# Smaller pieces of tensor work between the attention steps, and small vector work gathered in every fourth step

## The chip, the core and the metric

The kernel runs on one core of one Trainium2 chip. The metric is the device time of one execution in microseconds (us), the median of several runs. The kernel before takes 1864.74 us (three runs, 1863.59 to 1865.54). One execution was profiled as well: it took 1867.24 us, and its recorded span is 1865.5 us.

A core has engines that each run their own instructions strictly in the order in which the program lists them, and that wait for one another only through semaphores: PE (TensorE, matrix products; PEld is its loading of weights), DVE (VectorE), ACT (ScalarE), POOL (GpSimd) and SP (SyncE, which here only issues DMA transfers). Matrix products land in PSUM, a small memory of eight banks.

## What is computed

The reference is a block of cross attention and a feed-forward part whose weights come from a table of 16 values. Cut to what matters:

```python
# x: (16, 256, 512), ctx: (16, 256, 512), mask: (16, 1, 512), float32
xn = layernorm(x)                                   # over the last axis
q = einsum('oc,bct->bot', Wq, xn) + bq              # 16 heads of 16 rows
k = einsum('oc,bcs->bos', Wk, ctx) + bk
v = einsum('oc,bcs->bos', Wv, ctx) + bv
dot = einsum('bhdt,bhds->bhts', q, k) / 4
m = mask[:, :, :, None] * mask[:, :, None, :]
a = softmax(m * dot - (1 - m) * 1e6, -1) * m
x = x + einsum('bhts,bhds->bhdt', a, v).reshape(16, 256, 512)
y = layernorm(x)
gate, up = y @ lut[gate_idx].T, y @ lut[up_idx].T   # 512 -> 1376
x = x + (silu(gate) * up) @ lut[down_idx].T         # 1376 -> 512
```

## The kernel before

The attention is cut into 64 units `u` of four heads each; two units make a group `k` (half of the 256 channels of one batch element `b`, so two groups make a batch element). A unit has eight steps, and the whole attention is one loop over steps `s`, from -46 to 513, with the order written out by hand. One step lists, in this order:

1. `scores_max(s + 16)`: two products `pa` of 512 columns for the unit that is two ahead, and one DVE reduction of their 1024 columns (L476), which gives the row maxima.
2. what the list `between[s]` holds, which `pe(...)` fills: work with matrix products in it.
3. `scores_exp(s)`: two products `pb` and one ACT exponential of 1024 columns (L493).
4. what the list `after[s]` holds, which `at(...)` fills: other work.
5. `looked.fill(...)`: some DVE instructions of the table look-up of the weights, counted in credits; a look-up instruction on 512 columns costs 0.15 + 512/1250 = 0.56 credits. The attention loop carries eight look-ups of 19 such instructions, which use up their credits near step 355.

Since an engine keeps the listed order, an instruction that waits holds back everything listed behind it on its engine. `pa` and `pb` share a pool of three PSUM tiles, taken in turn: `pb` of step n+1 takes the tile of `pa` of step n, so it waits for that reduction, and `pa` of step n+2 takes the tile of `pb` of step n, so it waits for that exponential. All other products of the attention use one bank, `ps_m`, and the output of a unit one more.

Work of a group `k`, with t = 16k, counted in steps: the products of q and k (`project`, two of 512 columns each), evicted by ACT, multiplied by the mask on POOL (L388), split into a high and a low part by ACT and POOL (`halve`, L394 and L396), written to memory by SP (`stage`) and fetched back in another layout into one of four QK tiles (`fetch_unit`); the products of v (`project_v`, four of 256 columns), evicted by ACT (L444), and then on POOL two additions of the bias (L447) and four products with the mask (L454). A unit's maxima are split on DVE (`halve_max`, L499 and L500), turned on PE (`turn_max`) and sent into the QK tile by POOL (`send_max`). The exponentials are multiplied with v by `apply_v`, in steps 8u+5 and 8u+9, so in every step with s % 4 == 1: these are the steps with products of v. After them come, per group, the sums and their inverse (`take_sums`, `load_sums`, `invert` on DVE, `send_sums`, `spread_sums`), the rows' end on POOL (`finish_rows`: L574 and L575), the statistics of the second layer norm on DVE (`stats2`: L92 and L93, then four small POOL instructions L97 to L100), the normalised rows on POOL (`norm2`, L593), their four transposes on PE (`turn_rows`, L600) and the stores. `stats1` and `norm1` do the first layer norm of a batch element, every second group.

Two steps are equal if they differ by 16, so the place of all this is best read as s mod 16. Before the change `finish_rows` stands in step 7, `stats2` in step 9, the last piece of `project_v` in step 12.

In the steps below 0 the first groups are prepared and the QK tiles filled; the feed-forward part follows the loop.

Of the kernel before, what the change touches and what calls it, by code (L numbers as in the profile page):

```python
# [9 lines left out]
F32 = mybir.dt.float32  # L10
# [10 lines left out]
def kernel(  # L21
# [17 lines left out]
    nc = tc.nc  # L39
    P = 128  # L40
    B, C, T = x.shape
# [7 lines left out]
    NCC = C // P  # L49
    NK = B * NCC  # L50
    NU = 2 * NK
    NH = T // P
    NO = (INTER + P - 1) // P
    NB = NK // 4
    AHEAD = 16
    NSTEP = 8 * NU
    PARTS = ((0, 4 * P), (4 * P, 8 * P), (8 * P, INTER))
    NP = NO // 2
    HALF = T // 2
# [7 lines left out]
    ps_m = ctx.enter_context(tc.tile_pool(name="ps_m", bufs=1, space=PSUM))  # L67
# [19 lines left out]
    def words(t):  # L87
        return t.bitcast(F32)
# [146 lines left out]
    with ExitStack() as att:  # L235
# [9 lines left out]
        wv = ac.tile([P, NCC, C], F32, tag="wv", name="wv")  # L245
# [5 lines left out]
        m_d = dpool.tile([B, 4, 2, T], F32, tag="m_d", name="m_d")  # L251
# [47 lines left out]
        m8 = early.tile([P, 4, 2, T], F32, tag="m8", name="m8")[:B]  # L299
# [37 lines left out]
        def send_mask():  # L337
            nc.vector.tensor_copy(m8[:, 2:4, 0, :], m8[:, 0:2, 0, :])
            nc.vector.tensor_copy(m8[:, 1:4:2, 1, :], m8[:, 0:4:2, 1, :])

        def fill_tiles():
            nc.sync.dma_start(m_d, m8)
            for t in vas:
                nc.vector.memset(t, 1.0)
            nc.vector.memset(words(Ks[1]), 1.0)
# [21 lines left out]

        nat, parts = {}, {}

        def project(k, which, o):  # L370
            b, oc = divmod(k, NCC)
            cx, xn, mb = inp[b][:3]
            w, src_t = (wk, cx) if which == "k" else (wq, xn)
            if o == 0:
                parts[which] = ps_m.tile([P, 512], F32, tag="m", name=f"p{which}_{k}")
            ps = parts[which]
            nc.tensor.matmul(  # L377
                ps, w[:, o, oc, :], src_t[:, o, :], start=(o == 0), stop=(o == NCC - 1)
            )
            if o < NCC - 1:  # L380
                return
            t = p1.tile([P, T], F32, tag=f"nat{which}", name=f"nat{which}_{k}")
            if which == "k":
                nc.scalar.activation(t, ps, AF.Identity, bias=bkc[:, oc : oc + 1])  # L384
            else:
                nc.scalar.activation(t, ps, AF.Identity, bias=bqc[:, oc : oc + 1], scale=QK)  # L386
            eng = nc.vector if k == 0 else nc.gpsimd
            eng.tensor_tensor(t, t, mb, ALU.mult)  # L388
            nat[which, k] = t
# [36 lines left out]
                nat.pop(("q", k))  # L426
                nat.pop(("k", k))

        def project_v(k, i):
            b, half = divmod(k, 2)  # L430
            cx = inp[b][0]
            if i == 0:
                parts["v"] = ps_m.tile([P, 512], F32, tag="m", name=f"pv_{b}_{half}")
            ps = parts["v"]
            c = 2 * half + i
            for o in range(NCC):
                nc.tensor.matmul(  # L437
                    ps[:, i * C : (i + 1) * C], cx[:, o, c * P : (c + 1) * P], wv[:, o, :],
                    start=(o == 0), stop=(o == NCC - 1),
                )  # L440
            if i == 0:
                return
            vt = p1.tile([P, 2, C], F32, tag="vt", name=f"vt_{b}_{half}")
            nc.scalar.copy(vt, ps.rearrange("p (c n) -> p c n", n=C))  # L444
            va = vas[b % 2]
            for cc in range(2):
                nc.gpsimd.tensor_tensor(vt[:, cc], vt[:, cc], bvb, ALU.add)  # L447
            for cc in range(2):
                c = 2 * half + cc
                m = mcol[:, b * NCH + c : b * NCH + c + 1]  # L450
                v4 = vt[:, cc].rearrange("p (h e d) -> p e h d", e=2, d=D)
                a4 = va[:, c].rearrange("p (h e) d -> p e h d", e=2)
                for e in range(2):
                    nc.gpsimd.tensor_scalar(  # L454
                        a4[:, e, :, 16 * e : 16 * e + 16], v4[:, e], m, None, ALU.mult
                    )
# [75 lines left out]
        dens, rbs, rows2 = {}, {}, {}  # L532
# [60 lines left out]
            nc.gpsimd.tensor_scalar(xn, u, rstd, nmr, ALU.mult, ALU.add)  # L593
            rows2[k] = xn

        def turn_rows(k):
            xn = rows2.pop(k)
            pt = ps_m.tile([P, 512], F32, tag="m", name=f"pt_{k}")
            for h in range(NH):
                nc.tensor.transpose(  # L600
                    pt[:, h * P : (h + 1) * P], xn[:, h * P : (h + 1) * P], ident
                )
            xt = rpool.tile([P, T], F32, tag="xt", name=f"xt_{k}")
            nc.scalar.copy(xt, pt)
            rows2[k] = xt
# [9 lines left out]
        def at(s, fn, *args):  # L615
            after[s].append(lambda: fn(*args))

        def pe(s, fn, *args):
            between[s].append(lambda: fn(*args))

        for u in range(NU):
            for c in range(NCH):
                pe(8 * u + 5 + 4 * (c // 2), apply_v, u, c)
        for k in range(NK):
            t = 16 * k
            for i in range(2):
                pe(t - 46 + 2 * i, project, k, "k", i)
                pe(t - 42 + 2 * i, project, k, "q", i)
                pe(t - 22 + 2 * i, project_v, k, i)
            at(t - 41, halve, k, "k")  # L630
            at(t - 37, halve, k, "q")
            at(t - 37, stage, k, "k")
            at(t - 33, stage, k, "q")
            for e in range(2):
                u = 2 * k + e
                at(8 * u - 23, fetch_unit, u)
                at(8 * u - 8, halve_max, u)
                pe(8 * u - 7, turn_max, u)
                at(8 * u - 6, send_max, u)
            at(t + 12, take_sums, k, 0)  # L640
            at(t + 20, take_sums, k, 1)
            at(t + 20, merge, k)
            at(t + 24, load_sums, k)
            at(t + 28, invert, k)
            at(t + 29, send_sums, k)
            at(t + 34, spread_sums, k)
            at(t + 39, finish_rows, k)
            at(t + 41, stats2, k)
            at(t + 42, send_rows, k)
            at(t + 42, norm2, k)  # L650
            pe(t + 47, turn_rows, k)
            at(t + 50, send_turned, k)
        for b in range(1, B):
            at(max(-22, 32 * b - 58), load_b, b)
            at(max(-14, 32 * b - 50), stats1, b)
            at(max(-13, 32 * b - 48), norm1, b, nc.gpsimd)
        for h in range(8):
            at(2 * h - 13, spread_mask, h)

        at(-43, halve_mask, 0)  # L660
        at(-41, halve_mask, 1)
        at(-39, send_mask)
        at(-32, fill_tiles)
        pe(-31, turn_mask)
        at(-29, rest_of_constants)

        right.close()
        lp = right.enter_context(tc.tile_pool(name="lookup", bufs=1, side="right"))
        looked = Lookups(lp, [weight_job(*w) for w in wpieces[:8]])
        xms, ws = [None] * NM, {}  # L670

        for s in range(min(between), NSTEP + 2):
            if 0 <= s + AHEAD < NSTEP:
                scores_max(s + AHEAD)
            for fn in between.pop(s, ()):
                fn()
            if 0 <= s < NSTEP:
                scores_exp(s)
            for fn in after.pop(s, ()):
                fn()  # L680
            if 0 <= s < NSTEP - AHEAD - 4:
                looked.fill(0.24)
            if s == NSTEP - AHEAD - 4:
                looked.rest()
                right.close()
                rx = ctx.enter_context(
                    tc.tile_pool(name="first", bufs=1, side="right", reuse_waits="tile")
                )
                xms[0] = rx.tile([P, 2, 4, NH, P], F32, tag="x0", name="x_0")
            if s in (NSTEP - 14, NSTEP - 13):  # L690
                k = s - NSTEP + 14
                nc.sync.dma_start(xms[0][:, k], xT_d[k])
            if s in (NSTEP - 11, NSTEP - 10):
                load_w(rx, s - NSTEP + 11)
# [5 lines left out]
    with ExitStack() as ffn:  # L700
        ps = ffn.enter_context(
            tc.tile_pool(name="ps_ff", bufs=7, space=PSUM, reuse_waits="tile")
        )
# [9 lines left out]
        def down_job(o):  # L713
# [16 lines left out]
        looked = Lookups(  # L730
            lp, [weight_job(*w) for w in wpieces[8:]] + [down_job(o) for o in range(NO)]
        )
# [209 lines left out]
        for n, (p, m) in enumerate(order):  # L942
# [36 lines left out]
            q = max(p, 1) + 1  # L979
# [142 lines left out]
```

## Time and profile before

| what | value |
|---|---|
| median of three runs | 1864.74 us |
| the profiled execution, its own time | 1867.24 us |
| its span | 1865.5 us |
| steps below 0 | up to about 57 us |
| attention steps | about 57 to 1057 us |
| feed-forward part | about 1057 to 1865 us |
| DVE reduction of `pa` (L476) | 512 times, mean 1219 ns |
| ACT exponential (L493) | 512 times, mean 1024 ns |
| granted TensorE clock, mean | 0.996 |

The view of windows gives, for a stretch of the span, how long each engine was busy and the granted TensorE clock (1.00 is full speed). The timeline lists instructions by start, with the idle time of their engine before them and what ended it in brackets; instructions that follow each other closely are merged into one row, and matrix products overlap, so distances are best taken from start to start. The view of waits sums the idle times by what ended them.

### The profile page before, as it was taken

What the parts mean: (1) busy time and instruction counts of PE and PEld (TensorE: products, weight loads), DVE (VectorE), ACT (ScalarE), POOL (GpSimd) and SP (SyncE); (2) the same over time, 40 slices, a digit from 0 to 9 for tenths busy, and PEclk for the clock granted to TensorE, in tenths of its full rate; (3) what the DMA queues carried; (4) which work ended last, traced back from release to release, by engine and by line L of the source; (5) the groups of instructions that cost most, each with busy time, mean ns of one, the idle gap of its engine ahead of it and who ended that gap; (6) DMA issues with size and microseconds to landing.
All of it is one profiled execution on the core that took longest, in us unless ns stands there. A gap on an engine that the chain in (4) does not pass through costs nothing.

```text
span 1865.5 us, 21778 instructions
## 1 busy us (share of the span) xinstructions
PE 1792.9 (96%) x7281; PEld 990.9 (53%) x7281; DVE 1354.4 (73%) x1882; ACT 807.7 (43%) x1103; POOL 672.5 (36%) x918
## 2 busy tenths in 40 slices
PE   5999999999999999999999999999999999999999
PEld 2455555545554555555554444444444443888888
DVE  7889888888888888877777588878888844323222
ACT  1566666666666666666666622222222222000000
POOL 5546565656665566656554220000000000111111
PEclk9999999999999999999999999999999999999999
DMA  7655667676667667665755633122222215543521
GB/s 195 163 141 154 169 184 165 168 182 170 160 171 184 168 150 172 183 168 146 171 147 117 234 124 107 66 93 77 92 74 85 75 60 200 190 156 116 189 69 45
DMA packets 117807, 264.88 MB, mean 142 GB/s; under 512 B 25920, under 2 KB 35072, under 8 KB 107312
## 3 DMA queue, kind: packets, MB, share of 16 engines
q1 hardware_dynamic: 103680, 249.04, 46.4%
q0 software_dynamic: 12672, 12.94, 3.8%
q10 hardware_dynamic: 1344, 1.52, 0.3%
q8 instruction: 58, 0.95, 0.2%
q14 instruction: 53, 0.43, 0.1%
HBM read 167.06 MB, written 91.03 MB: 138 GB/s over the span
## 4 chain that ended last, share of the span: by engine, by line
PE 76%; DVE 10%; ACT 6%; DMA 5%; issue 2%; SPq 0%; POOL 0%; ACTq 0%; DVEq 0%
PE pv L523 10%; PE pb L489 9%; PE pa L472 9%; PE pb_g L737 6%; PE pb L737 6%; ACT pt L493 6%; PE pb_u L737 5%; PE px L737 4%; DVE nm L476 4%; PE pe L737 4%; PE pa_g L737 4%; PE pe_g L737 4%; PE pe_u L737 4%; PE pa_u L737 3%; PE pk L377 3%; DMA QK<-dk 2%
## 5 line engine op out<-in xcount | busy, mean ns | idle before, releaser
L476 DVE TENSOR_REDUCE nm<-pa 128x2 f32<-128x1024 f32 x512 | 619.9, 1219 | 161.6 <-PE pa L472 158.5
L493 ACT ACTIVATE pt<-pb 128x1024 f32<-128x1024 f32 x512 | 515.0, 1024 | 229.5 <-PE pb L489 229.1
L489 PE MATMUL pb<-QK 128*128 128x512 f32 x1024 | 401.1, 474 | 22.6 <-ACT pt L493 14.6
L472 PE MATMUL pa<-QK 126*128 126x512 f32 x1024 | 340.1, 414 | 30.1 <-ACT pt L493 21.4
L489 PEld LDWEIGHTS pb<-QK 128*128 128x128 f32 x1024 | 175.5, 190 | 177.4 <-DVE nm L476 66.4
L523 PE MATMUL pv<-pt,va 128*32 128x512 f32 x2048 | 249.2, 601 | 0.2 <-ACT pt L493 0.2
L472 PEld LDWEIGHTS pa<-QK 126*128 126x128 f32 x1024 | 182.0, 190 | 125.6 <-ACT pt L493 75.4
L850 POOL DMA_DIRECT2D h<-ht_g x8 | 4.2, 529 | 473.0 <-DVE ht_g L861 465.1
L523 PEld LDWEIGHTS pv<-pt,va 128*32 128x32 f32 x2048 | 54.0, 109 | 124.9 <-issue 117.6
L1042 POOL TENSOR_TENSOR ob<-u2d,xr 128x256 f32<-128x256 f32 x16 | 19.5, 1219 | 210.9 <-DVE u2d L1039 210.9
L388 POOL TENSOR_TENSOR natk<-natk,mb 128x512 f32<-128x512 f32 x31 | 40.0, 1289 | 136.4 <-ACT natk L384 136.4
L737 PE MATMUL px<-wd,hs 128*128 128x256 f32 (+1 forms) x384 | 88.2, 379 | 0.0
L816 ACT COPY pb_g<-pa_g 128x512 f32<-128x512 f32 (+1 forms) x24 | 13.6, 569 | 170.9 <-PE pa_g L737 170.9
L1028 ACT COPY pb<-px 128x256 f32<-128x256 f32 x16 | 5.7, 357 | 185.8 <-PE px L737 185.8
L454 POOL TENSOR_SCALAR va<-vt,mcol 128x128 f32<-128x128 f32 x128 | 78.5, 632 | 0.0
L737 PEld LDWEIGHTS px<-wd,hs 128*128 128x128 f32 (+1 forms) x384 | 73.0, 190 | 10.5 <-issue 0.5
L377 PE MATMUL pk<-ctx,wk 128*128 128x512 f32 x128 | 69.0, 624 | 8.9 <-DVE wk L319 7.5
L1039 DVE TENSOR_TENSOR u2d<-pe,u2d 128x256 f32<-128x256 f32 x16 | 6.8, 424 | 97.2 <-PE pe L737 97.2
L529 ACT COPY us<-pv 128x512 f32<-128x512 f32 x64 | 37.5, 586 | 86.1 <-PE pv L523 70.9
L377 PE MATMUL pq<-xn,wq 128*128 128x512 f32 x128 | 69.9, 632 | 2.4 <-ACT natk L384 1.7
L737 PE MATMUL pb_g<-xt,wg 128*128 128x512 f32 (+1 forms) x144 | 68.0, 594 | 2.1 <-DVE sg_g L835 2.1
L437 PE MATMUL pv<-wv,ctx 128*128 128x256 f32 x256 | 67.9, 389 | 0.8 <-ACT natq L386 0.8
(208 smaller groups left out, 2888.6 us busy)
## 6 DMA issues: line engine op xcount, KB each, us to landing
QK<-dk SPq DMA_DIRECT2D x128, 256.0 KB
QK<-dq SPq DMA_DIRECT2D x252, 128.0 KB
h<-ht_u SPq DMA_DIRECT2D x80, 256.0 KB
hs<-h SPq DMA_DIRECT2D x8, 2560.0 KB
dk<-hlk SPq DMA_DIRECT2D x32, 512.0 KB
dq<-hlq SPq DMA_DIRECT2D x32, 512.0 KB
ctx<-in_ctx_dram SPq DMA_DIRECT2D x16, 512.0 KB
xn<-in_x_dram SPq DMA_DIRECT2D x16, 512.0 KB
```

What stands on the lines that cost most here:

```text
L377: nc.tensor.matmul(ps, w[:, o, oc, :], src_t[:, o, :], start=(o == 0), stop=(o == NCC - 1))
L388: eng.tensor_tensor(t, t, mb, ALU.mult)
L437: nc.tensor.matmul(ps[:, i * C : (i + 1) * C], cx[:, o, c * P : (c + 1) * P], wv[:, o, :], start=(o == 0), stop=(o == NCC - 1),)
L454: nc.gpsimd.tensor_scalar(a4[:, e, :, 16 * e : 16 * e + 16], v4[:, e], m, None, ALU.mult)
L472: nc.tensor.matmul(pa[:, jj, :], q[0:126, j, c * P : (c + 1) * P], kt[0:126, j, :], start=True, stop=True,)
L476: nc.vector.tensor_reduce(nms[u][:, h : h + 2, c], pa, AX.X, ALU.max, negate=True)
L489: nc.tensor.matmul(pb[:, jj, :], kt[:, j, c * P : (c + 1) * P], q[:, j, :], start=True, stop=True,)
L493: nc.scalar.activation(pts[u, c][:, h : h + 2, :], pb, AF.Exp)
L523: nc.tensor.matmul(accs[u][32 * j : 32 * j + 32, :], va[:, c, 8 * oc + 2 * j + e, :], pt[:, j, :], start=(c == 0), stop=(c == NCH - 1),)
L529: nc.scalar.copy(us[u], accs.pop(u))
L737: nc.tensor.matmul(out, lhs[i], rhs[i], start=(first and i == 0), stop=(last and i == n - 1), skip_group_check=True,)
L1042: nc.gpsimd.tensor_tensor(obs[0][:, HALF:], u2, xr[0][:, HALF:], ALU.add)
```

## The change

Each product of q and k is cut into two of 256 columns, so that a group has four pieces for q and four for k; the four products of v become four pieces; the four transposes of a group's rows become two and two. They are spread so that each step without products of v has one piece (a few have two). DVE's small work moves into steps with products of v: `halve_max` goes from step 8u-8 to 8u-7, behind that step's reduction; the look-ups come every fourth step with four times the credit; `invert`, `stats1` and, with them, `send_sums`, `spread_sums` and `finish_rows` move by one step. `stats2` stays. Modulo 16 the last piece of v now stands in step 8, ahead of `finish_rows`, which moves from step 7 to step 8; q is projected in steps 10 to 14, split in step 1 and stored in step 5. At the start the mask's store, the fills, the loads of batch element 1 and the fetch of unit 1 trade places.

POOL's order in a period of 16 steps is, before, from step 4: L388 for k, sums, L574 and L575, L396 for k, L388 for q, sums, L97 to L100, L593, `send_max`, L396 for q, L447, L454, and so on. After it is, from step 4 (by the kernel's line numbers before): L388 for k, sums, L396 for k, L447 twice, L454 four times, L574, L575, sums, L97 to L100, L593, `send_max`. DVE's order at step 9 is, after: reduction, L499, L500, L92 and L93 of `stats2`, look-ups, reduction of step 10.

```diff
             nc.vector.tensor_copy(m8[:, 2:4, 0, :], m8[:, 0:2, 0, :])
             nc.vector.tensor_copy(m8[:, 1:4:2, 1, :], m8[:, 0:4:2, 1, :])
 
+        def store_mask():
+            nc.sync.dma_start(m_d, m8)
+
         def fill_tiles():
-            nc.sync.dma_start(m_d, m8)
             for t in vas:
                 nc.vector.memset(t, 1.0)
             nc.vector.memset(words(Ks[1]), 1.0)
...
 
         nat, parts = {}, {}
 
-        def project(k, which, o):
+        def project(k, which, i):
             b, oc = divmod(k, NCC)
             cx, xn, mb = inp[b][:3]
             w, src_t = (wk, cx) if which == "k" else (wq, xn)
-            if o == 0:
+            if i == 0:
                 parts[which] = ps_m.tile([P, 512], F32, tag="m", name=f"p{which}_{k}")
             ps = parts[which]
+            half, o = divmod(i, NCC)
+            at = slice(half * HALF, half * HALF + HALF)
             nc.tensor.matmul(
-                ps, w[:, o, oc, :], src_t[:, o, :], start=(o == 0), stop=(o == NCC - 1)
+                ps[:, at], w[:, o, oc, :], src_t[:, o, at], start=(o == 0), stop=(o == NCC - 1)
             )
-            if o < NCC - 1:
+            if i < 2 * NCC - 1:
                 return
             t = p1.tile([P, T], F32, tag=f"nat{which}", name=f"nat{which}_{k}")
             if which == "k":
...
                 nat.pop(("q", k))
                 nat.pop(("k", k))
 
-        def project_v(k, i):
+        def project_v(k, n):
             b, half = divmod(k, 2)
             cx = inp[b][0]
-            if i == 0:
+            if n == 0:
                 parts["v"] = ps_m.tile([P, 512], F32, tag="m", name=f"pv_{b}_{half}")
             ps = parts["v"]
+            i, o = divmod(n, NCC)
             c = 2 * half + i
-            for o in range(NCC):
-                nc.tensor.matmul(
-                    ps[:, i * C : (i + 1) * C], cx[:, o, c * P : (c + 1) * P], wv[:, o, :],
-                    start=(o == 0), stop=(o == NCC - 1),
-                )
-            if i == 0:
+            nc.tensor.matmul(
+                ps[:, i * C : (i + 1) * C], cx[:, o, c * P : (c + 1) * P], wv[:, o, :],
+                start=(o == 0), stop=(o == NCC - 1),
+            )
+            if n < 2 * NCC - 1:
                 return
             vt = p1.tile([P, 2, C], F32, tag="vt", name=f"vt_{b}_{half}")
             nc.scalar.copy(vt, ps.rearrange("p (c n) -> p c n", n=C))
...
             nc.gpsimd.tensor_scalar(xn, u, rstd, nmr, ALU.mult, ALU.add)
             rows2[k] = xn
 
-        def turn_rows(k):
-            xn = rows2.pop(k)
-            pt = ps_m.tile([P, 512], F32, tag="m", name=f"pt_{k}")
-            for h in range(NH):
+        def turn_rows(k, half):
+            xn = rows2[k]
+            if half == 0:
+                parts["t"] = ps_m.tile([P, 512], F32, tag="m", name=f"pt_{k}")
+            pt = parts["t"]
+            for h in range(2 * half, 2 * half + 2):
                 nc.tensor.transpose(
                     pt[:, h * P : (h + 1) * P], xn[:, h * P : (h + 1) * P], ident
                 )
+            if half == 0:
+                return
             xt = rpool.tile([P, T], F32, tag="xt", name=f"xt_{k}")
             nc.scalar.copy(xt, pt)
             rows2[k] = xt
...
             between[s].append(lambda: fn(*args))
 
         for u in range(NU):
+            pe(8 * u - 7, halve_max, u)
             for c in range(NCH):
                 pe(8 * u + 5 + 4 * (c // 2), apply_v, u, c)
         for k in range(NK):
             t = 16 * k
-            for i in range(2):
-                pe(t - 46 + 2 * i, project, k, "k", i)
-                pe(t - 42 + 2 * i, project, k, "q", i)
-                pe(t - 22 + 2 * i, project_v, k, i)
+            for i in range(4):
+                pe(t - 46 + min(i, 2), project, k, "k", i)
+                pe(t - 38 + i + i // 3, project, k, "q", i)
+                pe(t - 26 + min(i, 2), project_v, k, i)
             at(t - 41, halve, k, "k")
-            at(t - 37, halve, k, "q")
             at(t - 37, stage, k, "k")
-            at(t - 33, stage, k, "q")
+            at(t - 31, halve, k, "q")
+            at(t - 27, stage, k, "q")
             for e in range(2):
                 u = 2 * k + e
-                at(8 * u - 23, fetch_unit, u)
-                at(8 * u - 8, halve_max, u)
+                at(8 * u - 23 if u != 1 else -22, fetch_unit, u)
                 pe(8 * u - 7, turn_max, u)
                 at(8 * u - 6, send_max, u)
             at(t + 12, take_sums, k, 0)
             at(t + 20, take_sums, k, 1)
             at(t + 20, merge, k)
             at(t + 24, load_sums, k)
-            at(t + 28, invert, k)
-            at(t + 29, send_sums, k)
-            at(t + 34, spread_sums, k)
-            at(t + 39, finish_rows, k)
+            at(t + 29, invert, k)
+            at(t + 30, send_sums, k)
+            at(t + 35, spread_sums, k)
+            at(t + 40, finish_rows, k)
             at(t + 41, stats2, k)
             at(t + 42, send_rows, k)
             at(t + 42, norm2, k)
-            pe(t + 47, turn_rows, k)
-            at(t + 50, send_turned, k)
+            pe(t + 47, turn_rows, k, 0)
+            pe(t + 48, turn_rows, k, 1)
+            at(t + 51, send_turned, k)
         for b in range(1, B):
-            at(max(-22, 32 * b - 58), load_b, b)
-            at(max(-14, 32 * b - 50), stats1, b)
-            at(max(-13, 32 * b - 48), norm1, b, nc.gpsimd)
+            at(max(-21, 32 * b - 58), load_b, b)
+            at(max(-15, 32 * b - 51), stats1, b)
+            at(max(-14, 32 * b - 48), norm1, b, nc.gpsimd)
         for h in range(8):
-            at(2 * h - 13, spread_mask, h)
+            at(2 * h + 1, spread_mask, h)
 
         at(-43, halve_mask, 0)
         at(-41, halve_mask, 1)
         at(-39, send_mask)
-        at(-32, fill_tiles)
+        at(-32, store_mask)
+        at(-26, fill_tiles)
         pe(-31, turn_mask)
-        at(-29, rest_of_constants)
+        at(-25, rest_of_constants)
 
         right.close()
         lp = right.enter_context(tc.tile_pool(name="lookup", bufs=1, side="right"))
...
                 scores_exp(s)
             for fn in after.pop(s, ()):
                 fn()
-            if 0 <= s < NSTEP - AHEAD - 4:
-                looked.fill(0.24)
+            if 0 <= s < NSTEP - AHEAD - 4 and s % 4 == 1:
+                looked.fill(0.96)
             if s == NSTEP - AHEAD - 4:
                 looked.rest()
                 right.close()
```

## The prediction, made before the change was run

> **What bounds the kernel now.** The page comes first.
>
> ```profile
> PE 1792.9 (96%) x7281; PEld 990.9 (53%) x7281; DVE 1354.4 (73%) x1882; ACT 807.7 (43%) x1103; POOL 672.5 (36%) x918
> ...
> PE 76%; DVE 10%; ACT 6%; DMA 5%; issue 2%; SPq 0%; POOL 0%; ACTq 0%; DVEq 0%
> ```
>
> The change leaves the feed-forward part alone, so only the attention steps, 57 to 1057 us, matter. How long is a period of 16 steps? L593 runs once in each:
>
> ```profile
> 175.82 0.77 POOL L593 TENSOR_SCALAR xn<-us,rs,nr 128x512 f32<-128x512 f32 x1
> 747.58 0.77 POOL L593 TENSOR_SCALAR xn<-us,rs,nr 128x512 f32<-128x512 f32 x1
> ```
>
> The next after 747.58 is at 778.64, 31.06 later; between the two shown lie 18 periods of 571.76/18 = 31.76 us. Next, one period's timeline (on PE, then ACT, DVE and POOL):
>
> ```profile
> 444.62 0.64 PE L472 MATMUL pa<-QK 126*128 126x512 f32 x2
> ...
> 445.96 0.73 PE L472 MATMUL pa<-QK 126*128 126x512 f32 x2 [0.23 <-ACT pt L493]
> ...
> 447.86 0.63 PE L472 MATMUL pa<-QK 126*128 126x512 f32 x2
> ...
> 450.84 0.63 PE L472 MATMUL pa<-QK 126*128 126x512 f32 x2
> ...
> 452.64 0.63 PE L472 MATMUL pa<-QK 126*128 126x512 f32 x2
> ...
> 451.84 1.28 POOL L574 TENSOR_TENSOR us<-us,rb 128x512 f32<-128x512 f32 x1 [1.68 <-DMA rb<-dd]
> ...
> 453.19 1.66 POOL L575 TENSOR_TENSOR us<-us,xr 128x512 f32<-128x512 f32 x1
> ...
> 459.49 0.68 DVE L92 BATCH_NORM_STATS2 bn_f<-us 128x6 f32<-128x512 f32 x1
> ...
> 460.30 1.19 DVE L476 TENSOR_REDUCE nm<-pa 128x2 f32<-128x1024 f32 x1
> ...
> 463.75 0.59 ACT L444 COPY vt<-pv 128x512 f32<-128x512 f32 x1
> ...
> 465.19 1.42 POOL L447 TENSOR_TENSOR vt<-vt,bvb 128x256 f32<-128x256 f32 x2
> ...
> 466.59 2.84 POOL L454 TENSOR_SCALAR va<-vt,mcol 128x128 f32<-128x128 f32 x4
> ```
>
> From `pa` to `pa` a step with products of v takes 450.84 - 447.86 = 2.98 us, one with a 512-column product of q 452.64 - 450.84 = 1.80, and a bare one 445.96 - 444.62 = 1.34, though its four products of about 0.465 each pair need only 0.93: it ends by waiting for the exponential. PE's own need for a projection is 1.80 - 0.93 = 0.87. The period adds up: 4 x 2.98, 4 x 1.80 (q, k), 2 x 1.80 (v: `pa` 458.87 to 460.68), about 1.45 with the transposes, 5 bare ones at about 1.4: 31.2.
>
> Last, the statistics at 459.49 start 4.6 us after L575 ended (454.85). That distance is what the change spends.
>
> **Evening out the pieces.** Nothing is added on PE: a piece of 256 columns has its row in today's v products, four instructions at 458.87 to 460.68 for two of them, so 0.435 each. A period needs 4 x 2.98 + 12 x 0.93 + 12 x 0.435 + 0.44 (four transposes: 943.60 to 944.50 less `pb`'s 0.46) = 28.7 us. A step with one piece takes 1.37, more than ACT's 1024 ns plus about 0.1, so the waits of bare steps go: worth 31.76 - 28.7 = 3.0 us a period in the look-up steps, 2.4 later. More weight loads are hidden (PEld is busy 53%). I keep 0.7 of waits with look-ups, 0.4 without: step 13 gives DVE `invert` (0.34 + 0.78), every second time `stats1` (1.6), and one or two look-ups of about 0.6 behind one reduction of 1.13, against some 2.8 us to the next one. Bounds 0.2 and 1.5.
>
> **DVE behind POOL at step 9.** This decides. `stats2` stays in step 9, but its input now comes out of POOL's step 8, behind the whole work on v. Take as zero PE's end of the last v piece in step 8.
>
> - ACT has the exponential of step 7 and L394 (0.62) in front of L444 (0.59). By the order of starts L394 ends near 0.4 and L444 near 1.0. POOL then does L396 for k (1.29) until 1.7.
> - L447 1.42, L454 2.37 (2.84 in the row above): 5.5. L574 and L575 1.28 + 1.30: about 8.2. (In 448 to 455 they took 3.0.)
> - DVE, held since about 2.1 to 4 behind `halve_max`, does L92 and L93, 460.30 - 459.49 = 0.81: 9.05. On average 1.71 look-ups (0.96/0.56) of 0.6: 10.1. Reduction of step 10: 11.3.
> - PE meanwhile: `pb` of 8 (0.46), step 9 (2.98), step 10 (1.37), `pa` and q piece of 11 (0.9): it is ready for `pb` of step 11 at 5.7, and that needs the PSUM tile of step 10's `pa`.
>
> So PE waits 5.6 us, 4.5 without look-ups, plus 0.1 to restart (0.57 instead of 0.47 to the next start after an idle PE). `halve_max` (0.34 alone; 0.85 + 1.20 at 961.95 beside POOL work) may stop PE first, at `turn_max`; that only splits the wait. Bounds: 4.3 (L444 by 0.7, L396 out of the way, one look-up) and 6.8 (L454 at 2.84, L574 and L575 at 3.0, two look-ups). Behind DVE's wait stand all later reductions; SP also waits, with the store of the rows (L579), and behind it the next k store and fetch, which have seven steps of margin.
>
> **The clock after the wait.** PE idle costs more than itself. The windows:
>
> ```profile
> 40.00:50.00 10.00, 6.14 (x13) 3.11 (x14) 5.22 (x7) 1.56 (x3) 5.69 (x7) 0.72 0.98 207
> ...
> 1040.00:1046.00 6.00, 3.90 (x20) 1.57 (x22) 0.88 (x2) 3.88 (x4) 1.75 (x5) 0.88 1.06 324
> 1046.00:1052.00 6.00, 5.81 (x32) 2.17 (x24) 0.55 (x2) 4.31 (x5) 2.13 (x4) 0.84 0.57 186
> ```
>
> The third column from the end is the granted clock. After 3.86 us of idle at 41.5 it is at half from 44.4 for 6.8 us (0.72 over 10 us is 5.6 us at half, and 0.88 from 50 to 55 is 1.2 more); after 2.10 us at 1041.3 for 3.4 us (0.12 x 6 x 2 + 0.16 x 6 x 2). A wait of 5.7 us should do the same every period: 3.4 to 6.8 us at half, part of it idle; I take 4.6 us of work at half, which loses 2.3. Bounds 0.5 and 3.4.
>
> The Trainium skill ("TensorE: Matmul & The Clock Gate", section "HAM oscillation — how this bites in real kernels") puts the limit at idle gaps over some 3.4 us and the way back at one busy window of as much. Here 2.10 us was enough, so the row is the stricter. By the page's figures the loss would be an estimated 1.7 us a period, and the sum 17 us less.
>
> **The rest.** At the start the fetch of unit 1 goes ahead of the loads of batch element 1: DVE's 3.70 us of idle before 46.64 can go, but `stats1` behind two reductions then waits for x, which comes later through DMA rings that were full (0.99 in 30 to 46 us). Zero, bounds -4 and +4. q's store (step 5) now leads its fetch (step 9) by four steps, 7 us, and the scores by eleven: zero, up to 0.5 a period.
>
> **Sum.** Both groups' work is there in periods 2 to 29. Twenty of them have look-ups: 28.7 + 5.7 + 2.3 + 0.7 = 37.4, against 31.76: +5.6 each, 113. Eight have none: 28.7 + 4.6 + 2.3 + 0.4 = 36.0 against 31.06: +4.9 each, 40. Four others gain 2: -8. Together +145 on the span, 2010; the profiled run was 2.5 us above the median, so 1865 + 145 = 2010 us.
>
> **Rivals.**
>
> - Faster: POOL ends L575 before DVE comes to it. Then only the evening out is left: (3.0 - 0.7) x 22 + (2.4 - 0.4) x 10 = 71, about 1794. It decides once L575 ends within about 2.6 us of the last v piece instead of 8.2. For it speaks that POOL is busy only 36%; against it that L447 and L454 alone take 3.8 and cannot start before the piece is evicted. 6%.
> - The wait is there but small, at 3.0 us, with the clock held: 28.7 + 3.1 + 0.6 = 32.4, +0.64 x 20 + 1.3 x 8 - 8 = +15, 1880. For it: gaps of up to 0.9 us in a clock window leave the clock at 1.00 today. Against: it needs 2.6 us less than the listed rows. 9%.
> - The change doesn't do what it says: if the exponential still sets all steps, evening gains nothing and the wait costs 8 a period, 28 x 8 = 224 more, 2089. Against it: steps of 1.80 show no idle. 5%.
>
> **Numbers.** My forecast has 80%: 2010 us. At the low bounds (28.7 + 4.4 + 0.5 + 0.2 = 33.8 and 32.7) +2.0 x 20 + 1.6 x 8 - 12 = +41, 1906; at the high (40.5 and 39.0) +8.7 x 20 + 7.9 x 8 + 4 = +241, 2106. All bounds at one end at once are unlikely, so the range is 1920 to 2090. A measurement tells about 0.2% (4 us) from none. Slower 0.92, same 0.02, faster 0.06.
>
> **What would show it.** Right: DVE's L92 of the rows waits some 4 to 6 us for POOL's L575 (L579 in the new lines) once a period, PE's `pb` waits for DVE 28 times by 3 us or more, the granted clock in the attention falls to about 0.9, bare-step waits for ACT fall from their present 75.4 us on PEld and 21.4 on PE (view of waits). Wrong: L575 ended before DVE's reduction of step 9, or PE idle but the clock at 1.00.

## The result, and the profile after

The changed kernel takes 2017.53 us (four runs, 2016.32 to 2022.28) against 1864.16 us of the kernel before beside it: a ratio of 1.0827, 95% interval 1.0808 to 1.0846. It is slower by 153 us; the forecast was 2010 us, range 1920 to 2090.

Of the kernel before, the granted clock in 40 slices of the span, and two groups of instructions, with busy time, mean ns, then the idle time just before them and what ended most of it:

```profile
PEclk9999999999999999999999999999999999999999
...
L489 PE MATMUL pb<-QK 128*128 128x512 f32 x1024 | 401.1, 474 | 22.6 <-ACT pt L493 14.6
...
L92 DVE BATCH_NORM_STATS2 bn_f<-us 128x6 f32<-128x512 f32 x32 | 21.7, 679 | 6.5 <-POOL us L575 6.5
```

The same of the changed kernel, behind the busy times of its engines:

```profile
PE 1831.8 (91%) x7537; PEld 1071.3 (53%) x7537; DVE 1309.9 (65%) x1882; ACT 811.5 (40%) x1103; POOL 674.8 (33%) x918
...
PEclk8998999989989989989999999999999999999999
...
L493 PE MATMUL pb<-QK 128*128 128x512 f32 x1024 | 420.6, 495 | 125.1 <-DVE nm L480 115.1
...
L92 DVE BATCH_NORM_STATS2 bn_f<-us 128x6 f32<-128x512 f32 x32 | 22.2, 694 | 151.1 <-POOL us L579 116.6
```

PE was busy 96% and is busy 91%. What is new stands in the last three rows: DVE sat idle 151 us in front of the row statistics (6.5 before), mostly until POOL's L579 (L575 before), and PE sat idle 125 us in front of `pb` (22.6 before), mostly until a DVE reduction. DVE's 151 us are 28 waits of 4.6 to 4.9 us, one a period, and one of 13.5 us behind the last of them. The page puts seven of the 28 down to a DMA, but each of the 28 ends within 0.04 us of the end of L579. The clock, at 9 in every slice before, drops to 8 in several slices.

Two successive ends of a period, from POOL's timeline:

```profile
376.06 0.76 POOL L597 TENSOR_SCALAR xn<-us,rs,nr 128x512 f32<-128x512 f32 x1
413.59 0.76 POOL L597 TENSOR_SCALAR xn<-us,rs,nr 128x512 f32<-128x512 f32 x1
```

They are 37.53 us apart; the mean of the six from 188.36 to 413.59 is 37.54. In the steps without look-ups (900 to 1115 us) the mean is 214.99/6 = 35.83.

One such period around step 9, from the timeline (start, length, engine):

```profile
477.93 1.28 POOL L400 TENSOR_TENSOR hlk<-natk,hlk 128x512 fp32r<-128x512 f32 x1 [5.24 <-ACT hlk L398]
...
479.18 1.40 POOL L451 TENSOR_TENSOR vt<-vt,bvb 128x256 f32<-128x256 f32 x2
...
480.58 2.35 POOL L458 TENSOR_SCALAR va<-vt,mcol 128x128 f32<-128x128 f32 x4
...
482.91 1.26 POOL L578 TENSOR_TENSOR us<-us,rb 128x512 f32<-128x512 f32 x1
...
484.25 1.26 POOL L579 TENSOR_TENSOR us<-us,xr 128x512 f32<-128x512 f32 x1
485.55 0.69 DVE L92 BATCH_NORM_STATS2 bn_f<-us 128x6 f32<-128x512 f32 x1 [4.92 <-POOL us L579]
...
487.26 2.35 DVE L480 TENSOR_REDUCE nm<-pa 128x2 f32<-128x1024 f32 x2
...
488.53 1.22 PE L493 MATMUL pb<-QK 128*128 128x512 f32 x2 [4.76 <-DVE nm L480]
489.55 1.05 PE L476 MATMUL pa<-QK 126*128 126x512 f32 x2
```

Read from top to bottom this is the forecast's list: POOL goes through L400, the work on v and the rows' end without a gap; DVE has been waiting for 4.92 us when L579 ends at 485.51; two look-ups and one reduction later PE gets its tile, after 4.76 us of idle (the row of L480 joins two reductions; the first ends at 488.48). The products of PE behind it take 1.05 us and more a pair instead of 0.63: the clock is at half.

The windows behind the same wait one period earlier, where PE resumed at 449.96 after 4.44 us of idle (start:end, length, busy time of PE, PEld, DVE, ACT and POOL; third column from the end: granted clock):

```profile
450.00:456.00 6.00, 6.00 (x18) 3.53 (x22) 3.63 (x4) 2.05 (x2) 2.13 (x4) 0.51 0.10 33
456.00:462.00 6.00, 5.45 (x30) 2.93 (x22) 5.48 (x11) 3.39 (x4) 3.69 (x6) 1.00 0.02 4
```

For six microseconds PE is busy all the time, but at half clock: 18 matmuls where the next six, at full clock, hold 30.

### The profile page after: what moved, and what is told of

The parts are those of the page before. It is cut to its first block, busy times and chain, and to the rows that moved or that the text cites. A ratio compares the mean times of both kernels' runs of the same rounds, so it can differ in the third digit from the quotient of the medians.

```text
span 2015.5 us, 22434 instructions
## 1 busy us (share of the span) xinstructions
PE 1831.8 (91%) x7537; PEld 1071.3 (53%) x7537; DVE 1309.9 (65%) x1882; ACT 811.5 (40%) x1103; POOL 674.8 (33%) x918
## 4 chain that ended last, share of the span: by engine, by line
PE 70%; DMA 8%; DVE 8%; POOL 5%; SPq 3%; issue 2%; ACT 2%; POOLq 0%; DVEq 0%; ACTq 0%
PE pb L493 10%; PE pa L476 9%; PE pv L527 8%; PE pb_g L747 6%; PE pb L747 5%; PE pb_u L747 5%; PE px L747 4%; PE pe L747 4%; PE pa_g L747 3%; PE pe_g L747 3%; PE pe_u L747 3%; DMA QK<-dq 3%; PE pa_u L747 3%; DVE nm L480 3%; DMA QK<-m_d 2%
## 5 line engine op out<-in xcount | busy, mean ns | idle before, releaser
L480 DVE TENSOR_REDUCE nm<-pa 128x2 f32<-128x1024 f32 x512 | 620.2, 1223 | 214.0 <-PE pa L476 209.6
L493 PE MATMUL pb<-QK 128*128 128x512 f32 x1024 | 420.6, 495 | 125.1 <-DVE nm L480 115.1
L476 PE MATMUL pa<-QK 126*128 126x512 f32 x1024 | 358.3, 434 | 19.5 <-DVE nm L480 9.2
L493 PEld LDWEIGHTS pb<-QK 128*128 128x128 f32 x1024 | 188.9, 203 | 221.2 <-DVE nm L480 148.9
L476 PEld LDWEIGHTS pa<-QK 126*128 126x128 f32 x1024 | 190.6, 205 | 105.9 <-ACT pt L497 56.3
L92 DVE BATCH_NORM_STATS2 bn_f<-us 128x6 f32<-128x512 f32 x32 | 22.2, 694 | 151.1 <-POOL us L579 116.6
L381 PE MATMUL pq<-xn,wq 128*128 128x256 f32 x256 | 90.6, 445 | 1.5 <-ACT natk L388 0.8
L400 POOL TENSOR_TENSOR hlk<-natk,hlk 128x512 fp32r<-128x512 f32 x31 | 39.6, 1276 | 152.3 <-ACT hlk L398 152.3
L381 PE MATMUL pk<-ctx,wk 128*128 128x256 f32 x256 | 73.8, 394 | 13.8 <-DVE wk L319 7.5
L400 POOL TENSOR_TENSOR hlq<-natq,hlq 128x512 fp32r<-128x512 f32 x31 | 39.6, 1278 | 131.8 <-ACT hlq L398 131.8
L458 POOL TENSOR_SCALAR va<-vt,mcol 128x128 f32<-128x128 f32 x128 | 76.4, 605 | 0.1
L392 POOL TENSOR_TENSOR natq<-natq,mb 128x512 f32<-128x512 f32 x31 | 39.6, 1278 | 104.2 <-ACT natq L390 99.1
```

What stands on the lines that cost most here:

```text
L92: nc.vector.bn_stats(st, xt)
L381: nc.tensor.matmul(ps[:, at], w[:, o, oc, :], src_t[:, o, at], start=(o == 0), stop=(o == NCC - 1))
L400: eng.tensor_tensor(hl[:, 1, :], t, words(hl[:, 0, :]), ALU.subtract)
L458: nc.gpsimd.tensor_scalar(a4[:, e, :, 16 * e : 16 * e + 16], v4[:, e], m, None, ALU.mult)
L476: nc.tensor.matmul(pa[:, jj, :], q[0:126, j, c * P : (c + 1) * P], kt[0:126, j, :], start=True, stop=True,)
L480: nc.vector.tensor_reduce(nms[u][:, h : h + 2, c], pa, AX.X, ALU.max, negate=True)
```

## Experiments

Line numbers in the runs are those of the changed kernel, shifted by up to five where a run adds or drops lines. Each run was timed beside the kernel before on the same chip, which took 1865.8 to 1867.3 us in these batches and 1864.16 beside the changed kernel, so 3 us between batches mean nothing.

**Take the wait away: `finish_rows` one step earlier.** It goes back to step 7, where it stands ahead of POOL's work on v.

```diff
-            at(t + 40, finish_rows, k)
+            at(t + 39, finish_rows, k)
```

> finish_rows goes back one step, to step 7, ahead of POOL's work on v; nothing else. Theory (DVE waits for POOL at the row statistics, and the clock drops after it): the wait of DVE's L92 for L579 falls from 5 us a period to under 0.5, the clock stays at 1.00, and only the evening out is left: about 1865 - 71 + 3 (later start) = 1797 us. Rival (the split products or the gathered DVE work cost the time themselves): stays above 1950.

Measured: 1845.78 us (ratio to before 0.9889, 0.9872 to 0.9905). DVE waits for L579 in front of the row statistics once (13.8 us, as the 13.5 at the end of the changed kernel) instead of in every period, and the group of `pb` reads

```profile
L493 PE MATMUL pb<-QK 128*128 128x512 f32 x1024 | 395.6, 468 | 11.4 <-ACT pt L497 6.1
```

PE's idle time in front of `pb` is 11.4 us instead of 125.1. So one line moved by one step is worth 172 us of the 2017.5: the wait and what follows it. The rival, that the pieces or the gathered DVE work cost the time, is out. But the sum expected 1797; evening out gains 21 us, not 68.

**Change POOL's order alone.** `finish_rows` stays in step 8 and is listed ahead of the work on v.

```diff
-            at(t + 40, finish_rows, k)
+            pe(t + 40, finish_rows, k)
```

> finish_rows stays in step 8 but is listed ahead of the work on v, so that only POOL's order changes. Theory: L579 ends about 4.3 us after the last v piece instead of 8.2; PE's wait falls to about 1.6 us with look-ups and 0.6 without, the clock holds: 28.7 + 1.7 + 0.7 and 28.7 + 0.7 + 0.4 a period, about 1837 us. Rival (one step is too little whatever POOL's order): near 2017.

Measured: 1873.82 us (1.0033, 1.0022 to 1.0045). From the view of waits (us in total, times, longest):

```profile
DVE bn_f L92 <- POOL us L579: 45.9, 27, 15.1
...
PE pb L493 <- DVE nm L480: 26.5, 28, 1.7
```

DVE's 45.9 us are 26 waits of 1.2 us and one of 15.1 behind them, which the first experiment has too (13.8). The step is the same as in the changed kernel, only the order on POOL differs, and 144 us are gone. DVE's wait falls from 4.92 to 1.19 us a period, by 3.73: what made the wait long is the 3.75 us of L451 and L458 in front. The 28 us to the first experiment are about what PE still waits (26.5), one step being short even so. Against the expected 1837 the miss is 37 us; the first experiment, which rests on the same sum for evening out, missed by 49.

**Keep the wait, keep the clock.** Ten products more in front of the waiting `pb`, in the half of the bank that q's third and fourth piece write afterwards; they are extra work without a use.

```diff
+            if which == "q" and i == 1:
+                for _ in range(10):
+                    nc.tensor.matmul(
+                        ps[:, HALF:], w[:, 0, oc, :], src_t[:, 0, HALF:], start=True, stop=True
+                    )
```

> Ten more products of 256 columns (4.35 us at full clock) stand in step 11 of each group in which q is projected, in front of the product that waits for DVE; they go to a half of the PSUM bank that is overwritten later. DVE's wait for POOL stays. Theory that the wait is followed by a loss of 2.3 us a period through the clock: the clock stays at 1.00, 28 x 2.3 = 64 us less, about 1953 us, though PE does 130 us more work. Rival (the clock costs nothing, all 8 us are the wait): 2017 or more.

Measured: 1975.7 us (1.0584, 1.0568 to 1.06), 41.8 us less than without the extra products. The window of 100 us that has a clock of 0.90 in the changed kernel:

```profile
400.00:500.00 100.00, 97.40 (x508) 61.29 (x508) 73.55 (x94) 59.30 (x75) 55.36 (x76) 1.00 0.56 146
```

The clock is at 1.00, and DVE still waits for POOL, 136.7 us in 26 waits, all but one of them about 5 us. So PE, with 77 us more of busy time, ends earlier: the idle time itself costs a second time, through the clock. The net gain is 41.8/28 = 1.5 us a period, where the forecast had 2.3; but the extra products cost time of their own. The first `pb` comes at 65.8 us instead of 60.5, and without look-ups ten products (4.48 us at 443.33 to 447.81) are longer than the wait of 3.84 that they fill. In the look-up steps, where they fit into it, eighteen periods take (836.17 - 198.81)/18 = 35.41 us each instead of (864.39 - 188.36)/18 = 37.56: 2.1 less.

**What each half of the change is worth.** First the pieces alone, with DVE's moves undone:

```diff
-            pe(8 * u - 7, halve_max, u)
+                at(8 * u - 8, halve_max, u)
-            at(t + 29, invert, k)
+            at(t + 28, invert, k)
...
-            at(t + 40, finish_rows, k)
+            at(t + 39, finish_rows, k)
...
-            if 0 <= s < NSTEP - AHEAD - 4 and s % 4 == 1:
-                looked.fill(0.96)
+            if 0 <= s < NSTEP - AHEAD - 4:
+                looked.fill(0.24)
```

> The pieces and the later q stay; the moves of DVE's small work (halve_max, look-ups, invert, stats1 and what hangs on them, finish_rows too) are undone. If evening out the pieces makes the gain: 1800 to 1815 us. If gathering DVE's work is needed for it (a look-up of 0.6 and a reduction of 1.13 in a step of 1.37 would hold PE): 1840 or more.

Measured: 1849.37 us (0.9907, 0.9888 to 0.9926). That lies in the range of the second expectation, but only because the first experiment itself fell short of its sum: against its 1845.78 it is 3.6 us more, with intervals that overlap (0.9872 to 0.9905 there), so the pieces bring nearly all of the gain without the gathered DVE work. Then the reverse, the kernel before with DVE's moves only:

```diff
+            pe(8 * u - 7, halve_max, u)
-                at(8 * u - 8, halve_max, u)
-            at(t + 28, invert, k)
+            at(t + 29, invert, k)
...
-            if 0 <= s < NSTEP - AHEAD - 4:
-                looked.fill(0.24)
+            if 0 <= s < NSTEP - AHEAD - 4 and s % 4 == 1:
+                looked.fill(0.96)
```

> The kernel before with only DVE's moves (halve_max, look-ups in every fourth step, invert, stats1, send_sums, spread_sums one step later); pieces, finish_rows and the start as before. If evening PE's work is what gains and the DVE moves alone are worth little: 1855 to 1870 us. If they carry e1's gain: below 1850.

Measured: 1869.81 us (1.0019, 1.001 to 1.0029). The pieces gain 17 us, DVE's moves lose 4 on their own, and on top of the pieces they bring nothing that is clear of the noise.

**Why evening out gives 21 us only: the statistics?** The first experiment's periods alternate (29.91, 31.40, 29.84, 31.38 between 617 and 740 us). On top of it, the statistics move.

```diff
-            at(max(-15, 32 * b - 51), stats1, b)
-            at(max(-14, 32 * b - 48), norm1, b, nc.gpsimd)
+            at(max(-15, 32 * b - 43), stats1, b)
+            at(max(-14, 32 * b - 42), norm1, b, nc.gpsimd)
```

> As e1, and stats1 goes from step 13 to step 5 of the next half period, norm1 right behind it (step 6), still ahead of q's products in step 10. If the two bn_stats pairs (1.6 us every second period) beside invert and the look-ups make the longer of e1's alternating periods (31.4 against 29.8): all near 29.8, 14 x 1.6 = 22 us less than e1, about 1823 us. Rival (the long periods come from POOL's norm1 or from DMA): within 5 us of e1.

Measured: 1847.43 us (0.9905, 0.9892 to 0.9919), the same as the first experiment. From the first `pb` to the last (62.8 to 1030.5) it takes 967.7 us against 970.6 there (60.8 to 1031.4), but it starts 2 us later. The time lies within the rival's 5 us, but the trace shows that what is gained in one step is in part lost in another. Step 15 of the period at 623 us, from `pa` to `pa`, took 2.98 us in the first experiment, and 1.41 in this run's at 622. But step 9 of the next period grows from 3.37 to 3.95. There PE waits at the turn of the maxima, 24.6 us in 31 waits of the whole run instead of 14.4 in 29:

```profile
549.50 0.27 PE L511 MATMUL pmx<-ident,hl 128*32 128x128 f32 x1 [1.38 <-DVE hl L504]
579.61 0.27 PE L511 MATMUL pmx<-ident,hl 128*32 128x128 f32 x1 [0.33 <-DVE hl L504]
```

In step 9 of each period PE waits there for `halve_max`, 0.3 us in one period and mostly 0.8 to 1.4 in the next, in which the statistics, and `norm1` on POOL, now stand ahead of it. So this run doesn't clear the statistics.

**`halve_max` back in step 8u-8**, with the last experiment's move kept for all batch elements but the second (`b` = 1), and `finish_rows` in step 7 as there:

```diff
-            pe(8 * u - 7, halve_max, u)
+                at(8 * u - 8, halve_max, u)
...
+            at(32 * b - 43 if b > 1 else -15, stats1, b)
+            at(32 * b - 42 if b > 1 else -14, norm1, b, nc.gpsimd)
```

> As e1, with halve_max back in step 8u-8, so that it no longer stands between a reduction and the turn of the maxima, and with stats1 in step 5 for all batch elements but the first (e5's move). If the 0.3 to 1.4 us that PE waits for halve_max in one of two units, together with the statistics, make the difference between e1's 30.3 us a period and PE's own 28.7: about 0.9 us a period less, 28 us, 1818 us. Rival (the rest is the exponential's pace and the steps with two pieces): within 8 us of e1's 1846.

Measured: 1835.12 us (0.9831, 0.9807 to 0.9855). PE's waits for L504 fall to 3.5 us in all. Of the expected 28 us against the first experiment 11 are gained, so that the result lies between the forecast and the rival. Against the run before it is 12; some 2 of them are the start, where the first `pb` is back from 62.8 to 60.9. With the statistics in step 5, then, `halve_max` behind the reduction cost about 10 us. Whether putting it back would gain as much with the statistics where the change has them was not tried.

**The start.** Two runs. One, on top of the run with the statistics moved, moves the loads of batch element 1 to step -36 and four fills from DVE to POOL:

```diff
+        for t in (words(Ks[1]), *vas, words(Ks[2])):
+            nc.gpsimd.memset(t, 1.0)
...
-            at(max(-21, 32 * b - 58), load_b, b)
+            at(32 * b - 58 if b > 1 else -36, load_b, b)
```

> As e5, and at the start the loads of batch element 1 go out behind the first store (step -36) and four fills move from DVE to POOL, which is idle there. If the loads' late place makes the later first exponential (product at 60.8 us in e1, 56.9 before): 57 us or earlier, so 4 us or more less than e5. Rival (the fetch of unit 0 sets it): as e5.

Measured: 1847.57 us (0.9904, 0.989 to 0.9917), as the run that it builds on, with the first `pb` at 63.9 instead of earlier. A miss: with the fills on POOL, DVE's normalisations of x took 6.5 us longer (last section), so this run doesn't show what the loads' place is worth by itself. The other puts the old order of the first loads back, on top of the run with `halve_max` back:

```diff
-                at(8 * u - 23 if u != 1 else -22, fetch_unit, u)
+                at(8 * u - 23, fetch_unit, u)
-            at(max(-21, 32 * b - 58), load_b, b)
+            at(max(-22, 32 * b - 58), load_b, b)
-            at(32 * b - 43 if b > 1 else -15, stats1, b)
-            at(32 * b - 42 if b > 1 else -14, norm1, b, nc.gpsimd)
+            at(32 * b - 43 if b > 1 else -14, stats1, b)
+            at(32 * b - 42 if b > 1 else -13, norm1, b, nc.gpsimd)
```

> As e8, with the first loads in the order of the kernel before (fetch of unit 1 in step -15, loads of batch element 1 in step -22). If their new order makes the later first exponential (60.8 against 56.9): 4 us less than e8. Rival (the later projection of q does): as e8.

Measured: 1828.49 us (0.9805, 0.9792 to 0.9819), 6.6 us less, though the two intervals overlap by a little (0.9807 and 0.9819). The first `pb` comes at 56.8 instead of 60.9, as expected, and the last at 1016.1 instead of 1020.4. It is the fastest version: 2.0% under the kernel before (1.8 to 2.1) and 189 us under the changed one.

## Why the prediction was right, point by point

- **DVE behind POOL at step 9.** Right, and decisive: removing it alone gives 172 us back. L579 was forecast to end 8.2 us after the last v piece; it ends at 485.51, and `pb`, the product behind that piece, starts at 477.31, so 8.2. PE's idle time before `pb` was forecast at 5.6 and 4.5 us, measured 4.76 (above; 4.65 on average of 18) and 3.85 (at 1078.54, without look-ups; 3.84 on average of eight). What was off is PE's own path: it came to that product 0.8 us later than the 5.7 worked out, of which 0.34 is the wait at the turn of the maxima, which the forecast had named as a split of the wait.
- **The clock.** Right in kind and in size: the span's mean clock is 0.953, and with PE kept busy 0.996. Behind each of the 28 waits the trace's clock is at half for 3.4 or 6.8 us. PE is busy in 132 us of this time, so that 66 us of work at full clock are lost, 2.4 a period; the forecast had 2.3. The prediction's lower estimate of 1.7 goes with 3.4 us at half, but 21 of the 28 stretches last 6.8. The run with the extra products agrees with its 2.1 in the look-up steps; its 1.5 over the whole span is net of what these products cost.
- **Evening out.** The mechanism exists, but this was the mis-sized term. The sum had 28.7 us a period plus 0.7 of waits (0.4 without look-ups). With the wait gone, in the first experiment, eighteen look-up periods (180.42 to 739.88) take 31.08 each and four later ones (800.51 to 920.60) 30.02. A good period of that run, step by step from `pa` to `pa`, has 3.42 at step 9 instead of 2.98 (`halve_max`), 1.39 and 1.26 in the steps with two transposes instead of 1.15 each, and 1.87 instead of 1.80 in each step with two pieces. Part of it is PE's own need: in the last run's four periods without look-ups

```profile
790.41:908.17 117.76, 117.76 (x640) 69.72 (x632) 92.19 (x105) 81.78 (x104) 76.13 (x109) 1.00 0.71 178
```

PE is busy without a gap, and they take 117.76/4 = 29.44 each, 0.7 more than the 28.7. With look-ups the same run takes 30.92 (174.49 to 731.05); no run isolates what makes these 1.5 us. The faster rival's price, 1794, was therefore 50 us too low, and the right figure for it is the 1846 of the first experiment.
- **Why the total came out.** 37.4 a period was forecast and 37.54 measured. Of the changed kernel's eighteen look-up periods

```profile
188.36:864.39 676.03, 578.71 (x2846) 341.03 (x2846) 466.44 (x593) 372.54 (x469) 354.57 (x486) 0.91 0.57 144
```

each takes 37.56 us, with PE busy 32.15 and idle 5.4. 5.0 of the busy time are at half clock, so 2.5 are lost and 29.6 are work at full clock. The forecast had 28.7 of work, 2.3 lost and 6.4 idle (5.7 and 0.7). The work was put 0.9 too low and the idle time 1.0 too high. That these cancel was luck of about 1 us a period, not insight. Without look-ups 36.0 was forecast and 35.83 measured, but the 31.06 that it was set against is a single period, and the shortest thereabouts: the six from 778.64 to 967.70 of the kernel before average 31.51, so the sum had some 4 us too much there.
- **The start** was taken as zero with bounds of 4 us either way: the first `pb` comes at 60.5 instead of 56.9, within the bounds.
- **The other rivals.** The small wait with the clock held did not come: the wait was 3.8 to 5.0 us and the clock fell. Its price of 1880 is close to the 1873.82 of the run with POOL's other order, but by chance: PE waited at most 1.7 us a time there, not 3.0, and evening out gained less than the price assumed. That the change does not do what it says falls with the pieces-only run.

## What to carry to other kernels

When work is moved by a step, read the order on every in-order engine that it meets, not only the one it was moved for: here POOL had 67% of its time free, and still an instruction of 0.69 us on DVE waited 5 us in every period, because 5 us of other POOL work had come to stand between its input and the place where it was listed. The distance between a producer and an in-order consumer is slack that a profile shows (4.6 us before the change), and a change that spends it should be priced against what is put in between. A stall of TensorE can cost more than its length: here waits of 4 to 5 us cost about half as much again through the clock, and filling them, even with products that nobody uses, gained 42 us.

## What was not expected of the hardware

DVE's two normalisations of x (L281, 128x512 each) took 1.00 us in the changed kernel and 7.49 us in the run with the fills on POOL. First that run's timeline, DVE and then POOL:

```profile
11.48 7.49 DVE L281 TENSOR_SCALAR xn<-xn,rs,nr 128x512 f32<-128x512 f32 x2 [1.22 <-POOL nr L100]
...
11.39 1.79 POOL L330 MEMSET QK<- 128x2048 f32 x1
13.13 3.54 POOL L330 MEMSET va<- 128x2048 f32 x2
16.62 2.07 POOL L330 MEMSET QK<- 128x2048 f32 x1
```

The row of DVE joins two instructions. One runs from 11.48 to 16.95 and ends 0.28 us behind POOL's third fill (16.67); the other ends at 18.97, 0.28 us behind the fourth (18.69), which itself took 2.07 us instead of 1.79. So the first was held not for one fill but for three, then came its turn, and the second was held for the fourth. The Trainium skill ("SBUF — State Buffer", section "Who interferes with whom") says that a VectorE instruction in a two-port mode, which a `tensor_scalar` such as L281 can enter, contends with GpSimd for a shared port pair: whoever issues first has it for the whole instruction, and the other blocks. The times agree with such a lock, though no view here tells that L281 ran in that mode; and they show that three instructions in a row can pass before the other engine gets its turn. `halve_max` too takes longer beside POOL work, 0.65 us instead of 0.17 for L504 at 479.97 and 464.78 in the changed kernel; that the port is the cause there was not tested.
